# Two-layer convolution and attention kernel: row stores in five pieces, row loads in parts by ScalarE, last stores over three queues

## The chip, the cores and the metric

The kernel runs on one core of one Trainium2 chip. The metric is the device time in microseconds (us) of one execution. All data are float32. The engines are named as in the profile: PE (TensorE, matrix multiplications), DVE (VectorE), ACT (ScalarE), POOL (GpSimd) and SP (SyncE). DMAs are issued by SP, ACT and POOL, each in the order of its own instruction queue.

## The reference

The input x is 2 images of 256 channels and 64 x 64 pixels. Two layers follow each other.

```python
# layer 0: full attention over 4096 pixels, 8 heads of 32 channels, and a masked blend
q, k, v = proj(Wq, bq) / sqrt(32), proj(Wk, bk), proj(Wv, bv)
attn = softmax(einsum('bnd,bmd->bnm', q, k)); fuse = einsum('bnm,bmd->bnd', attn, v)
hybrid = conv1x1(concatenate([x, fuse]), Wf, bf)
x = hybrid * m + x * (1 - m)                      # m: the mask, resized to 64 x 64
# layer 1: a channel gate, attention in 8 x 8 windows, then two grouped convolutions
x = x * sigmoid(relu(x^T ca_w1 + ca_b1) ca_w2 + ca_b2)
x = x + window_attention(x)                       # 4 heads of 64 channels
x = channel_shuffle(x, 4)
y = relu(bn1(conv7x7(x, sa_w1, groups=64)))       # 256 -> 64 channels
y = bn2(conv7x7(y, sa_w2, groups=64))             # 64 -> 256 channels
return x * sigmoid(y)
```

## The kernel before

**Preparation** (some 177 us): projections q, k and v of both images go to DRAM; batch norm is folded into the convolutions' weights, and for each of the 16 *units* (4 of the 64 groups each) a banded weight matrix of 896 KB is built in DRAM (`w_s`).

**Attention** (up to 2674 us): an image is cut into 8 chunks of 512 pixels. For every chunk, two head groups and 32 key blocks give 1024 slots in all. A slot is scores on PE (L666), the exponential on ACT (L679), the product with v on PE (L718), and sums on DVE (L724). When a chunk is through, `stage` runs the rest of layer 0 and the window attention for it, in pieces between later slots. Its last piece adds the result up in `xo` (L1005) and stores its rows to `x_s` in DRAM (L1022). `x_s` holds the rows as the convolutions want them: 3 overlapping blocks of 32 rows per image (`BLOCKS`), 64 groups, 70 columns with the padding.

**Convolutions** (`convolve`): both 7 x 7 convolutions are matrix products with the banded weights. The work list is `items`: 26 pairs of a unit and the images that it takes. Items 0 to 9 are units 0 to 8 and 15 of image 0, which need nothing of the last chunk; they run between the pieces of the last chunk's `stage`. Items 10 to 16 are units 2 to 8 of image 1, items 17 to 22 are units 9 to 14 of both images (the *two-image units*), and items 23 to 25 are units 15, 1 and 0 of image 1.

One step k of the loop at the end of `convolve` is: `conv1(k + 1)`, `conv2(k)`, `gate(k)`, the loads of rows for a later item (`load_rows`), `store(k)`, and sometimes a load of weights (`load_w`). The order on each engine is that of the code.
- `conv1` of a one-image item: 56 matmuls (L1162), then a relu on ACT (L1170).
- `conv1_pairs` of a two-image item: 88 matmuls (L1125) that use sums of neighbouring weights (`both`) and differences of neighbouring columns (`dx`). The first matmuls have `both` as weights. ACT copies the middle sum out (L1136), DVE makes the two results (L1137, L1138), ACT does the relu (L1140).
- `differences(k + 1)` comes at the end of every `conv1(k)`: if the next item takes two images, DVE computes its `dx` from its rows (L1097) and its `both` from its weights (L1102).
- `conv2`: 112 matmuls (L1193) into two PSUM pairs of three, a tanh (L1204) and a scaling copy (L1212) on ACT for each image into a buffer z (four buffers).
- `gate`: z times x on DVE (L1224).
- `store`: 12 DMAs an image from z to the output (L1253; 24 KB or 16 KB each), dealt over queues by the list `engines`. Those for ACT are put in `held` and issued behind the next conv2's copies (L1251). Row loads that wait in `queue` go out on SP between the stores (L1249).

Rows of an item are loaded into one of six buffers (`xcs`) for items from 10 on. One-image items take three DMAs of 140 KB, two-image items two of 420 KB, all issued by SP. Step 12 asks for item 17's rows, step 13 for item 18's, and so on up to step 16 for item 21's; item 22's are asked for by step 17, itself a two-image step, and go out on SP at once (L1075).

For the last chunk the row stores are dealt over POOL and SP and cut into three ranges of groups: 8 to 20 (units 2 to 4), 20 to 64, 0 to 8. After the first range, `last_rows` loads the rows of items 10 to 12.

## Time and profile before

| | |
|---|---|
| median of 3 runs | 2883.06 us (2881.55 to 2884.48) |
| the profiled execution's own time | 2883.86 us |
| its span, from the first to the last instruction | 2882.0 us, mean granted TensorE clock 0.998 |
| busy: PE | 2852.5 us, 99% |
| busy: DVE, ACT, POOL | 2484.3 (86%), 2392.5 (83%), 576.9 (20%) |
| DMA | 305.65 MB, mean 106 GB/s |
| last matmul of attention, of the kernel | about 2674.3, 2868.7 |

Times in the text are us from the span's start. The page gives the busy time of each engine; a stretch of the span can be asked for by itself, and the timeline gives the instructions in order with the idle time before each and what ended it. SPq and ACTq stand for the sequencers of SP and ACT: there the DMA issues are shown, which do not count as busy. When a DMA has landed is told by the semaphore that it raises.

### The profile page before, as it was taken

To read this page: it belongs to the slowest core of one execution; us is meant where nothing else is said; L and a number is where in the kernel's file an instruction comes from. 1 tells how busy PE (TensorE), PEld (TensorE's weight loads), DVE (VectorE), ACT (ScalarE), POOL (GpSimd) and SP (SyncE) were. 2 spreads that over 40 slices of the span, in tenths; PEclk is the share of its full clock that TensorE was granted. 3 is DMA by queue.
4 is the path that set the end of the run, shared out by engine and by line. 5 is a ranking of instruction groups with operands and counts; after the bars stand their busy time and mean duration, and the time that the engine had idled before them with its cause. 6 is when DMAs were issued, how large, how long until landed. Compare 5 with 4: busy or idle time off the path is not lost.

```text
span 2882.0 us, 85464 instructions
## 1 busy us (share of the span) xinstructions
PE 2852.5 (99%) x37198; PEld 831.5 (29%) x37198; DVE 2484.3 (86%) x1374; ACT 2392.5 (83%) x3643; POOL 576.9 (20%) x948
## 2 busy tenths in 40 slices
PE   9999999999999999999999999999999999999998
PEld 4541122222222222222222222222222222222686
DVE  2349999899999999998999999999989899999423
ACT  5569979898888888898989888888989898888434
POOL 7111111111111212121121011111211110000376
PEclk9999999999999999999999999999999999999999
DMA  8555533333343434353333334333434432231675
GB/s 260 202 184 176 154 79 82 94 81 89 74 97 76 109 77 96 87 94 89 85 91 76 88 72 99 76 87 88 101 83 91 93 86 82 64 117 44 188 194 140
DMA packets 245906, 305.65 MB, mean 106 GB/s; under 512 B 121348, under 2 KB 137934, under 8 KB 245266
## 3 DMA queue, kind: packets, MB, share of 16 engines
q1 hardware_dynamic: 200058, 231.43, 28.1%
q0 software_dynamic: 40784, 65.90, 11.9%
q8 instruction: 294, 4.82, 0.7%
q10 hardware_dynamic: 4680, 2.76, 0.4%
q14 instruction: 90, 0.74, 0.1%
HBM read 221.88 MB, written 66.39 MB: 100 GB/s over the span
## 4 chain that ended last, share of the span: by engine, by line
PE 93%; DVE 3%; issue 2%; DMA 1%; POOL 1%; ACT 1%; SPq 0%; ACTq 0%; DVEq 0%; POOLq 0%
PE sa L666 36%; PE ava L718 34%; PE qka L552 4%; PE hya L552 4%; PE v L489 2%; PE c2a L1193 2%; PE vwa L552 2%; PE opa L552 2%; DVE suma L724 2%; PE k L450 2%; PE q L450 1%; PE c1a L1162 1%; PE sca L912 1%; PE oa L974 1%; POOL out_dram L1253 1%
## 5 line engine op out<-in xcount | busy, mean ns | idle before, releaser
L679 ACT ACTIVATE ea<-sa 128x512 f32<-128x512 f32 (+1 forms) x3072 | 2036.4, 747 | 46.3 <-PE sa L666 18.0
L666 PE MATMUL sa<-qa,ka 32*64 32x512 f32 x16384 | 1141.7, 613 | 2.1 <-DVE vst L501 1.7
L724 DVE TENSOR_TENSOR suma<-suma,ea 128x2048 f32<-128x2048 f32 x480 | 1096.4, 2284 | 5.2
L718 PE MATMUL ava<-ea,va 128*32 128x512 f32 x8192 | 1091.0, 605 | 0.3
L724 DVE TENSOR_TENSOR odda<-odda,ea 128x2048 f32<-128x2048 f32 x420 | 959.8, 2285 | 33.1 <-ACT ea L679 33.1
L666 PEld LDWEIGHTS sa<-qa,ka 32*64 32x64 f32 x16384 | 238.8, 129 | 796.6 <-ACT ea L679 728.8
L696 POOL DMA_DIRECT2D folda<-suma x336 | 235.6, 925 | 935.9 <-DVE suma L726 861.3
L718 PEld LDWEIGHTS ava<-ea,va 128*32 128x32 f32 x8192 | 161.4, 108 | 833.3 <-issue 804.3
L1022 POOL DMA_DIRECT2D xs<-xo x98 | 69.5, 718 | 925.3 <-DVE xo L1005 924.2
L1253 POOL DMA_DIRECT2D out_dram<-za x217 | 122.4, 572 | 51.4 <-DVE za L1224 24.5
L552 PE MATMUL qka<-ua,qkv_w 128*32 128x512 f32 x1024 | 115.7, 592 | 0.0
L887 ACT ACTIVATE qka<-qka,qkv_b 128x512 f32<-128x512 f32 x64 | 40.5, 683 | 75.4 <-PE qka L552 75.4
L469 DVE TENSOR_REDUCE top<-sq 128x128 f32<-128x2048 f32 x16 | 36.6, 2286 | 76.0 <-ACT sq L463 76.0
L808 ACT ACTIVATE ta<-hya,bf 128x512 f32<-128x512 f32 x32 | 20.3, 684 | 98.5 <-PE hya L552 98.5
L1193 PE MATMUL c2a<-yca,wa 32*64 32x192 f32 (+1 forms) x2912 | 84.8, 368 | 2.1 <-issue 1.7
L764 POOL DMA_DIRECT2D invs<-inva x62 | 34.8, 570 | 236.2 <-DVE inva L779 234.8
L724 DVE TENSOR_TENSOR suma<-ea,ea 128x2048 f32<-128x2048 f32 x32 | 73.1, 2285 | 7.6 <-ACT ea L679 7.6
L1204 ACT ACTIVATE za<-c2a 128x384 f32<-128x384 f32 x64 | 27.8, 487 | 61.2 <-PE c2a L1193 34.9
L1193 PEld LDWEIGHTS c2a<-yca,wa 32*64 32x64 f32 x2912 | 67.7, 191 | 18.0 <-issue 10.0
L726 DVE TENSOR_TENSOR suma<-suma,odda 128x2048 f32<-128x2048 f32 x30 | 68.8, 2292 | 1.0
L724 DVE TENSOR_TENSOR odda<-ea,ea 128x2048 f32<-128x2048 f32 x30 | 68.5, 2284 | 1.2 <-ACT ea L679 1.2
L552 PE MATMUL hya<-fa,WfT 128*32 128x512 f32 x512 | 59.6, 607 | 2.2 <-DVE fa L785 2.2
(167 smaller groups left out, 1581.1 us busy)
## 6 DMA issues: line engine op xcount, KB each, us to landing
ka<-ks SPq DMA_DIRECT2D x256, 256.0 KB
va<-vs SPq DMA_DIRECT2D x256, 256.0 KB
wa<-ws SPq DMA_DIRECT2D x17, 896.0 KB
ws<-zeros SPq DMA_DIRECT2D x16, 896.0 KB
folda<-suma POOLq DMA_DIRECT2D x224, 64.0 KB, 3.2
folda<-suma POOLq DMA_DIRECT2D x112, 128.0 KB, 4.4
xs<-xo POOLq DMA_DIRECT2D x76, 140.0 KB, 7.1
qs<-qst SPq DMA_DIRECT2D x16, 512.0 KB
```

The costliest lines, as they stand in the source:

```text
L450: nc.tensor.matmul(s[:, g, :], w[:, kc, g * P : (g + 1) * P], rhs, start=(kc == 0), stop=(kc == KC - 1),)
L489: nc.tensor.matmul(sv[:, m, :], xs0[i][:, kc, m * P : (m + 1) * P], wv[:, kc, :], start=(kc == 0), stop=(kc == KC - 1),)
L552: nc.tensor.matmul(out[o : o + 32], weights[:, o : o + 32], x, start=start, stop=stop)
L666: nc.tensor.matmul(heads[j][o], k[r, cols][:, o], q[r, g, :], start=True, stop=not shifted)
L679: nc.scalar.activation(e[:, h, :], tile, AF.Exp, scale=SCALE0)
L696: nc.gpsimd.dma_start(dst[p : p + rows], total[rows * k : rows * k + rows, h, :], accum_op=ALU.add if k else ALU.bypass,)
L718: nc.tensor.matmul(av[r, :], v[:, m % PB, r], e[:, j, :], start=start, stop=stop)
L724: nc.vector.tensor_add(total, first.pop(m % chains, total), e)
L726: nc.vector.tensor_add(acc[1], acc[1], acc[2])
L1022: eng.dma_start(x_s[b, n, p + r0 : p + r1, g0:g1].rearrange("r g w -> g r w"), xo[64 * h + g0 : 64 * h + g1, oc, r0 - WS * c : r1 - WS * c ...
L1193: nc.tensor.matmul(tiles[j // 2][o, j % 2, 0 : n * W], w[r, d, o], y[r, 0:n, d : d + W], start=(d == 0), stop=(d == KS - 1),)
L1253: eng.dma_start(*args)
```

## The change

It has three parts.
1. **Row stores of the last chunk.** The ranges of groups are now 8 to 20, 20 to 36, 36 to 48, 48 to 64 and 0 to 8. The first two are stored at once, with `last_rows` between them as before. The other three wait in `rows_later`, and one is stored behind each of the next three `store` calls (steps 6, 7 and 8 by the timeline of before).
2. **Rows of two-image items.** Where `load_x` put two DMAs into `queue`, it now puts six parts, one per image and block, into `fetch`. `fetch_rows(2)` lets ACT issue two of them at the end of `conv1`, of `conv1_pairs` and of `conv2`; `differences(k)` first has ACT issue what is left of item k.
3. **Last stores.** For the last four items the list of queues is written out letter by letter (g POOL, s SP, a ACT).

```diff
-            parts = [(UG * 2, UG * 5), (UG * 5, NG), (0, UG * 2)] if last else [(0, NG)]
-            for g0, g1 in parts:
+            def store_rows(g0, g1):
                 for oc in range(KC):
...
-                if last and g0 == UG * 2:
-                    staged[0](FIRST + 2)
+            if not last:
+                return store_rows(0, NG)
+            store_rows(UG * 2, UG * 5)
+            staged[0](FIRST + 2)
+            store_rows(UG * 5, UG * 9)
+            for part in ((UG * 9, UG * 12), (UG * 12, NG), (0, UG * 2)):
+                rows_later.append(part)
+            staged.append(store_rows)
...
                     elif len(images) == 2:
-                        queue.append((to, src))
+                        fetch.extend((k, to[:, n], src[:, n]) for n in range(nb))
...
+            def fetch_rows(n, k=-1):
+                while fetch and (n > 0 or fetch[0][0] <= k):
+                    nc.scalar.dma_start(*fetch.popleft()[1:])
+                    n -= 1
...
             def differences(k):
...
+                fetch_rows(0, k)
                 n = B * nb * UG * WP
...
+                fetch_rows(2)                  # conv1_pairs and conv1, ahead of:
                 differences(k + 1)
...
                 while held:
                     held.popleft()()
+                fetch_rows(2)                  # conv2
                 return zs
...
-                engines = (nc.gpsimd, nc.gpsimd, nc.sync)
-                if k == len(items) - 1:
-                    engines = (nc.scalar, nc.sync)
-                elif k == len(items) - 2:
-                    engines = (nc.sync, nc.scalar, nc.sync, nc.gpsimd)
-                elif k >= len(items) - 4 or len(images) == 2:
-                    engines = (nc.gpsimd, nc.sync)
+                last = k - len(items)
+                plan = {-1: "sasasasasass", -2: "sgsasgsasgsa", -3: "gsagsgasgasg", -4: "gsgsagsgsgsa"}
+                plan = plan.get(last, "gs" if len(images) == 2 else "ggs")
+                engines = [{"g": nc.gpsimd, "s": nc.sync, "a": nc.scalar}[i] for i in plan]
...
                 store(k, z, queue)
+                if rows_later:
+                    staged[1](*rows_later.popleft())
```

More of the change, by code (lines that the diff above doesn't have):

```diff
@@ L1033, in pipeline @@
         FIRST = EARLY + 1
-        staged, held = [], deque()
+        staged, held, rows_later, fetch = [], deque(), deque(), deque()
         def convolve():
@@ L1215, in conv2 @@
                     held.popleft()()
+                fetch_rows(2)
                 return zs
```

## The prediction

> **What bounds the kernel now.** I read the page's engine shares first (PE 99% busy), then busy times by stretch of the last 137 us, where all that the diff touches runs, then the timeline there, the waits and the chain. Columns: stretch, us, then busy us (and instructions) of PE, PEld, DVE, ACT, POOL, granted clock, DMA share, GB/s.

> ```profile
> 2745.00:2757.00 12.00, 10.78 (x368) 9.33 (x353) 2.06 (x3) 4.29 (x8) 9.24 (x16) 1.00 0.75 179
> 2757.00:2803.00 46.00, 44.39 (x1391) 38.19 (x1376) 12.99 (x14) 17.66 (x33) 39.52 (x70) 1.00 0.72 201
> 2803.00:2848.00 45.00, 45.00 (x1015) 34.57 (x1003) 20.71 (x27) 19.31 (x37) 28.71 (x51) 1.00 0.70 208
> 2848.00:2869.00 21.00, 20.46 (x624) 16.92 (x616) 5.91 (x8) 11.77 (x25) 19.90 (x36) 1.00 0.37 74
> 2869.00:2882.00 13.00, 0.00 (x0) 0.00 (x0) 1.10 (x3) 1.45 (x5) 1.39 (x3) 0.60 0.26 52
> ```

> TensorE is the bound up to its last matmul at 2868.7. It idles 1.2 us in the first row, 1.6 in the second and 0.5 in the fourth, most of it put down to "issue". In the third row, the two-image items, it never stops: whatever comes late there moves the end by as much. The last 13 us are stores and the exit. So there is little to win: 3.3 us of gaps and a part of the tail.

> The timeline about item 20, a two-image item, shows how short its preparation is:

> ```profile
> 2816.49 5.73 SPq L1253 DMA_DIRECT2D out_dram<-za  x10
> 2816.52 4.87 PE L1193 MATMUL c2a<-yca,wa 32*64 32x384 f32 x112
> 2817.29 1.90 DVE L1097 TENSOR_TENSOR dxa<-xea 128x1679 f32<-128x1679 f32 x1
> 2817.41 0.62 ACT L1140 ACTIVATE yca<-yta,cbias 128x384 f32<-128x384 f32 x1 [1.36 <-DVE yta L1138]
> 2819.11 0.58 DVE L1102 TENSOR_TENSOR botha<-wa 128x384 f32<-128x384 f32 x1
> 2821.32 0.99 PE L1125 MATMUL c1a<-xea,botha 128*32 128x192 f32 x16
> ```

> VectorE makes dx and both for item 20 from its rows (2817.29 to 2819.69, 2.40 in all). TensorE uses both as the very first weights of that item's first convolution, at 2821.32. The slack is 1.6 us. For item 19 it is 2.0 (both ends at 2810.34, PE starts at 2812.34). Now the rows are there many us earlier.

> **Rows by ScalarE.** For items 17 to 21, six parts of 140 KB each replace two SP loads of 420 KB. They enter `fetch` at steps 12 to 16, and two leave behind each conv1 and each conv2, four a step, from step 13. By the end of step 16, 16 of 30 have left: items 17 and 18 and four parts of 19. So:
> - the last two of 19 leave behind the relu of 18 (step 17), just ahead of differences(19);
> - of 20, two leave after conv2(17), two behind the relu of 19, and the last two are forced there by differences(20);
> - of 21 likewise behind the relu of 20.

> VectorE's subtraction needs all six parts. Those of 17 and 18 are out a whole conv half earlier or more; I cost them at nothing.

> When does the last part land? ScalarE's sequencer runs ahead: its event waits for the next instruction begin at 2817.42, as the relu starts. SP issues of such a part last 0.34 to 0.42; with 0.05 between, the fourth starts 1.3 after the relu, the second 0.45. Semaphore updates in the trace give the landing of SP's 140 KB loads: 2.15 at least (2730.89 to 2733.04), 2.2 to 2.75 with little beside, 3.5 to 4.1 beside stores and other loads, 5.6 to 7.1 behind an 896 KB weight load. The chain has one:

> ```profile
> 2702.90 3.27 DMA xea<-xs
> ```

> Counting from the end of the previous item's first convolution, TensorE wants the next after 4.73 us (2816.59 to 2821.32).
> - Item 19: relu +0.46 (2807.61 to 2808.07), second part +0.45, landing 4.3 (between 2.15 and 6.4, since SP has just sent 896 KB of weights and 840 KB of rows, on another queue), dx and both +2.40: 7.6, a stall of 2.9.
> - Item 20: +0.82, +1.3, landing 2.6 (only 24 KB stores beside it), +2.40: 7.1, a stall of 2.4.
> - Item 21: the same with landing 3.0 (the tail of item 23's load beside it): 7.5, a stall of 2.8.

> Sum +8.1. With 2.15 for every landing it is 0.7 + 2.0 + 2.0 = 4.7; with 6.4 for item 19 and 4.1 for the others 5.0 + 3.9 + 3.9 = 12.8. Behind VectorE's wait stand the gates of 17 to 19: gate(18) would start at 2823.7 instead of 2823.23, and only stores wait for it.

> [...]

> The issues themselves: 30 x 0.42 = 12.6 us of ScalarE's sequencer. Two behind a pair's last copy run under that copy (0.85). Up to four behind a relu (1.7) fall into the 3.4 to 3.8 us in which ScalarE waits for conv2. Cost 0; without this cover up to 12.6. SP loses ten issues (some 6 us in 2777 to 2801), where it had idle time: 0.

> **A wait that may come with them.** SP and ACT share eight landing semaphores in the trace, and an issue waits until the one eight before it has landed. At the start of the kernel this holds ScalarE up:

> ```profile
> 25.62 0.34 ACTq L477 DMA_DIRECT2D out_b<-in_out_b_dram  x1
> 28.80 1.26 ACT L460 ACTIVATE qst<-q,bq 128x512 f32<-128x512 f32 x2 [5.37 <-DMA out_b<-in_out_b_dram]
> ```

> By the times of before SP has issued five of its twelve stores at 2817.41, and the eighth before is a load that landed by 2816.3: no wait, 0. If all twelve count ahead of the fetch, its fourth part waits for the ninth store, landed at 2822.45: +3.8 for item 20 and again for 21.

> **Rows of the last chunk.** 12 DMAs become 20: POOL and SP get four more each. POOL: 4 x 0.65 (rows 0.57 to 0.73) = 2.6 us, spread over steps 6 to 8. POOL is busy 39.5 of 46 us there; behind it stand the output stores, and z has four buffers, so one is wanted again some 20 us later. SP: 4 x 0.3 to 1.2, with idle time behind. Item 13's rows are still stored at once, those of 17 on by step 8. Cost 0 to +1. The other way: PE's 1.22 us "issue" gap at 2754.4 lies beside the landing of the old burst (SP's row stores took 5.1 to 6.5); it may shrink. The three 420 KB loads beside it stay, so I take half: -0.6 (-1.2 to +1).

> **Last stores.** For the last four items SP has 30 stores now and 27 after, POOL 21 and 18, ACT 9 and 15.

> ```profile
> 2859.82 16.07 SPq L1253 DMA_DIRECT2D out_dram<-za  x28
> 2871.01 6.01 ACTq L1251 DMA_DIRECT2D out_dram<-za  x8
> ```

> SP runs without a break until 2875.9, and its own exit (2.7 to its first wait, 1.7 idle between two waits) sets the end; ScalarE's exit is done 1.4 earlier. SP's 3 issues less at 0.48 are -1.4. But SP and ACT together issue one per 0.38 here, each waiting for a landing eight back, and together they have three more: +1.1. ScalarE's four issues behind the eviction of 23 take 1.7 us from 2861.5; the relu of 25 started at 2863.1 and is wanted, 0.4 long, at 2865.6. I take -0.5 (-1.4 to +1.5). [...]

> **Sum.** +8.1 - 0.6 - 0.5 = +7.0. The profiled execution took 2883.86 (span 2882.0 and 1.9 around it), 0.8 above the median of 2883.06; on the median the forecast is 2890.1.

> **Rivals.**
> - *Not slower: the parts are early enough.* If the last parts of each item land before the slack is used up, no stall is left, and tail and gap give -1.1 to -2.6: about 2881. The point of decision: item 20's last part landed by 2818.9 (2821.3 less 2.40), 0.2 after its fourth issue. The fastest row is 2.15, so it needs half a step more of lead than I count. 5%, of which 2 reach the bound for faster.
> - *Short stalls.* Landings near 2.15 and the full gains: 4.7 - 2.6 to 4.7 + 1.0, 2885 to 2888.8. For it: ScalarE's queue is otherwise empty, so no weight load is ahead of the parts. Against: DMA share 0.70. 25%.
> - *The shared landings bind.* 8.1 + 7.6 - 1.1 = +14.6: 2897.7. For it: the start of the kernel. Against: the count of five stores. 18%.
> - My forecast, stalls of 7 to 11 us: 2888.9 to 2894, 52%.

> The measurement can tell about 0.2% (5.8 us) from no change. Faster by more would need 2877.3, almost all that gaps and tail hold, with no stall: 2%. Within 0.2%: 28%. Slower: 70%. The range 2885 to 2898 leaves out the first rival and more than a full lane wait.

> **What would show it.** Right: in the two-image stretch TensorE has three gaps of 2 to 3 us ahead of L1125 of items 19, 20, 21, released by VectorE's both, and VectorE's dx (L1097) waits on the DMA of the rows; none ahead of 17, 18 and 22. ScalarE issues thirty row parts, with no idle of its own behind them. Wrong: stretch still full of PE, or gaps elsewhere; ScalarE's evictions (L1204) waiting on row DMAs (third rival); a tail from the last matmul to the end that is not 12.3 to 14.8 us (13.3 now).

## The result and the profile after

The changed kernel took a median of 2899.68 us (2896.44 to 2903.76, six runs), the kernel before beside it 2883.02 (2881.55 to 2886.55, six runs): a ratio of 1.0053, 95% interval 1.0043 to 1.0063. That is slower by 16.7 us. The forecast was slower by 7.0 us, 2890.1, with a range up to 2898.0; the measured median lies above it.

The profiled execution took 2897.57 us, its span is 2895.8. The busy times by stretch, in the columns used above (last four: granted clock, DMA share, GB/s after the engines):

```profile
2745.00:2757.00 12.00, 10.26 (x336) 9.11 (x336) 1.52 (x3) 4.29 (x8) 9.98 (x18) 1.00 0.71 173
2757.00:2803.00 46.00, 43.82 (x1390) 38.74 (x1386) 13.80 (x15) 17.68 (x33) 39.77 (x71) 1.00 0.68 182
2803.00:2848.00 45.00, 33.48 (x645) 24.27 (x644) 15.20 (x20) 13.10 (x25) 21.89 (x40) 0.85 0.62 183
2848.00:2869.00 21.00, 21.00 (x488) 15.28 (x476) 6.78 (x9) 8.68 (x17) 13.01 (x24) 1.00 0.45 115
```

Most of the loss is in the third row, the two-image items. PE was busy 45.0 of 45.0 us there and is now busy 33.5, with 645 matmul records in place of 1015. The 11.5 us of idle time are not the whole: the granted clock has fallen from 1.00 to 0.85, so the remaining matmuls are longer too.

The timeline of PE gives the gaps, each ahead of the first convolution of a two-image item. The bracket holds the idle time before the instruction and what ended it; only the first matmuls of each item are shown:

```profile
2800.40 1.36 PE L1137 MATMUL c1a<-xla,botha 128*32 128x192 f32 x24 [1.29 <-ACT za L1218]
2815.05 2.16 PE L1137 MATMUL c1a<-xla,botha 128*32 128x192 f32 x24 [5.64 <-DVE botha L1114]
2828.98 2.17 PE L1137 MATMUL c1a<-xea,botha 128*32 128x192 f32 x24 [3.33 <-DVE botha L1114]
2841.98 1.76 PE L1137 MATMUL c1a<-xea,botha 128*32 128x192 f32 x24 [2.55 <-ACT za L1218]
2852.43 1.35 PE L1137 MATMUL c1a<-xla,botha 128*32 128x192 f32 x24
```

These are items 18 to 22, with gaps of 1.29, 5.64, 3.33, 2.55 and none: 12.8 us. Three of them were forecast, at 2.9, 2.4 and 2.8; the one ahead of item 18 was not. The first and fourth line name ACT as releaser, but VectorE's `both` ended within 0.1 us of PE's start there as well (item 18: 2799.74 and 0.56 long, PE at 2800.40). The first 24 matmuls take 1.35 us for item 22 and 2.16 for item 19 with the same shapes: that is the clock.

Where item 19's `both` was late, the timeline of all engines shows (the first line is the issue of item 20's first two parts):

```profile
2811.99 0.81 ACTq L1096 DMA_DIRECT2D xea<-xs  x2
2812.57 1.91 DVE L1109 TENSOR_TENSOR dxa<-xla 128x1679 f32<-128x1679 f32 x1 [7.56 <-DMA xla<-xs]
2814.40 0.55 DVE L1114 TENSOR_TENSOR botha<-wa 128x384 f32<-128x384 f32 x1
```

VectorE is idle for 7.56 us ahead of `dx`, which waits for rows, then makes `dx` and `both`, and PE starts at once. The chain of waits goes through the same DMA:

```profile
2800.40 3.13 PE c1a L1137 x62
2805.43 7.12 DMA xla<-xs
2812.57 0.07 DVE dxa L1109
```

The row part that ScalarE issued at 2805.43 landed 7.12 us later. The landing of the last part of each item, from the semaphore updates in the trace, with its issue: item 18 2791.99 and 5.90, item 19 2805.43 and 7.12, item 20 2822.65 and 3.72, item 21 2836.45 and 2.86.

The granted clock, asked for stretch by stretch, falls to one half at three of the gaps. The first three rows below are such stretches, the fourth lies between two of them:

```profile
2811.94:2818.76 6.82, 3.71 (x48) 2.62 (x52) 4.12 (x4) 0.86 (x2) 2.65 (x5) 0.50 0.26 66
2829.00:2832.42 3.42, 3.42 (x44) 2.45 (x48) 1.61 (x2) 0.07 (x1) 2.38 (x5) 0.50 0.94 317
2842.66:2846.07 3.41, 3.41 (x51) 2.87 (x47) 1.04 (x2) 0.20 (x1) 3.03 (x6) 0.50 0.64 193
2818.76:2829.00 10.24, 6.91 (x164) 4.75 (x156) 3.22 (x5) 4.19 (x8) 4.10 (x8) 1.00 0.59 164
```

The first convolutions of items 19, 20 and 21 take 5.79, 5.65 and 5.71 us for it, where item 22's takes 4.20 and those of the kernel before 4.25: 1.5 + 1.4 + 1.5 = 4.4 us.

At the end, the last conv2 waits for the relu of item 25, and that stands behind ScalarE's four stores of item 22:

```profile
2875.11 4.56 ACTq L1263 DMA_DIRECT2D out_dram<-za  x4
2879.72 0.42 ACT L1183 ACTIVATE yca<-c1a,cbias 128x192 f32<-128x192 f32 x1 [4.22 <-DMA out_dram<-za]
2880.19 2.98 PE L1207 MATMUL c2a<-yca,wa 32*64 32x192 f32 x112 [1.41 <-ACT yca L1183]
```

Four issues that should take 1.7 us last 4.56. The third and fourth start at 2878.16 and 2879.36, each within 0.08 us of the last update of the semaphore that it uses: they waited for the landing of an earlier store, 2.0 us in all. The second is 1.30 long, which no semaphore explains. PE waits 1.41 where it waited 0.28. The stores of SP:

```profile
2855.31 33.04 SPq L1265 DMA_DIRECT2D out_dram<-za  x51
```

SP runs without a break until 2888.35. From the last matmul's end (2883.17) to the end it is 12.6 us, 13.3 before.

**The account.** From the last attention matmul to the last matmul it was 194.4 us, and is 210.9: +16.5. Of that the gaps ahead of items 18 to 21 are 12.8, the half clock behind them 4.4, the wait of the last conv2 1.1, together 18.3; the remaining -1.8 are smaller gaps elsewhere, of which I can put none to an edit. With the tail at -0.65 it makes +15.9 behind attention, against 16.7 on the medians (interval 12.4 to 18.2). The two profiled spans differ by 13.8 only, since attention, which the change doesn't touch, ended 2.1 us earlier in the second.

### The profile page after: what moved, and what is told of

It reads as the page before. It is cut to its first block, busy times and chain, and to the rows that moved or that the text cites. A ratio compares the mean times of both kernels' runs of the same rounds, so it can differ in the third digit from the quotient of the medians.

```text
span 2895.8 us, 85471 instructions
## 1 busy us (share of the span) xinstructions
PE 2854.9 (99%) x37198; PEld 833.6 (29%) x37198; DVE 2484.6 (86%) x1374; ACT 2392.6 (83%) x3643; POOL 577.1 (20%) x949
## 4 chain that ended last, share of the span: by engine, by line
PE 92%; DVE 3%; issue 2%; DMA 2%; POOL 1%; ACT 1%; SPq 0%; DVEq 0%; ACTq 0%; POOLq 0%
PE sa L666 35%; PE ava L718 34%; PE qka L552 4%; PE hya L552 4%; PE v L489 2%; PE vwa L552 2%; PE opa L552 2%; DVE suma L724 2%; PE c2a L1207 2%; PE k L450 2%; PE q L450 1%; PE c1a L1175 1%; PE sca L912 1%; POOL out_dram L1265 1%; PE oa L974 1%
```

## The experiments

The first four kernels ran on one chip (kernel before there: 2885.82 median, 25 runs), the second four on another (2886.94, 15 runs). So the ratios are compared, not the times. The theory: ScalarE's parts leave too late, VectorE's `dx` waits, PE idles, and the idling halves the clock. The rivals: another of the three parts costs the time; the lead is enough and something else is late; the clock has no part in it.

### Each part alone

Row stores only: the other two parts as before.

```diff
-                        fetch.extend((k, to[:, n], src[:, n]) for n in range(nb))
+                        queue.append((to, src))
...
-                plan = {-1: "sasasasasass", -2: "sgsasgsasgsa", -3: "gsagsgasgasg", -4: "gsgsagsgsgsa"}
+                plan = {-1: "as", -2: "sasg", -3: "gs", -4: "gs"}
```

> The kernel before with only the row stores of the last chunk in five pieces. Theory A (the last parts of items 18 to 21 come late, and that is nearly the whole loss): 2883, within 2 us of the kernel before, no gap ahead of L1137 of items 18 to 21. Theory B (the pieces themselves or their queues cost several us): 2887 or more.

Measured: 2883.86, ratio 0.9994 (0.9985 to 1.0004). There is no gap ahead of items 18 to 21. From attention to the last matmul 196.0 us, tail (from there to the end) 13.9.

Row fetch by ScalarE only: three ranges of row stores and the old list of queues.

```diff
-            store_rows(UG * 5, UG * 9)
-            for part in ((UG * 9, UG * 12), (UG * 12, NG), (0, UG * 2)):
-                rows_later.append(part)
-            staged.append(store_rows)
+            store_rows(UG * 5, NG)
+            store_rows(0, UG * 2)
...
-                plan = {-1: "sasasasasass", -2: "sgsasgsasgsa", -3: "gsagsgasgasg", -4: "gsgsagsgsgsa"}
+                plan = {-1: "as", -2: "sasg", -3: "gs", -4: "gs"}
```

> The kernel before with only the two-image rows in parts by ScalarE. Theory A: +14 to +17 us over the kernel before, from gaps of 1.3, 5.6, 3.3 and 2.6 us ahead of items 18 to 21 (12.8 in all) and half a clock behind three of them (4.4). Theory B: less than +8, the rest being in the row stores and the last stores.

Measured: 2900.11, ratio 1.0051 (1.0034 to 1.0068), that of the whole change. The timeline of PE in this kernel has the same four gaps (line numbers are two lower):

```profile
2804.74 1.36 PE L1135 MATMUL c1a<-xla,botha 128*32 128x192 f32 x24 [1.58 <-ACT za L1224]
2818.75 2.17 PE L1135 MATMUL c1a<-xla,botha 128*32 128x192 f32 x24 [5.00 <-DVE botha L1112]
2833.38 1.34 PE L1135 MATMUL c1a<-xea,botha 128*32 128x192 f32 x24 [3.18 <-DVE botha L1112]
2846.30 1.34 PE L1135 MATMUL c1a<-xea,botha 128*32 128x192 f32 x24 [2.41 <-DVE botha L1112]
```

Together 12.2 us. The granted clock is 0.5 for 6.8 us about item 19 and for 3.4 us in item 20, and stays full behind the gap of 2.41.

Last stores only:

```diff
-            store_rows(UG * 5, UG * 9)
-            for part in ((UG * 9, UG * 12), (UG * 12, NG), (0, UG * 2)):
-                rows_later.append(part)
-            staged.append(store_rows)
+            store_rows(UG * 5, NG)
+            store_rows(0, UG * 2)
...
-                        fetch.extend((k, to[:, n], src[:, n]) for n in range(nb))
+                        queue.append((to, src))
```

> The kernel before with only the new deal of the last stores. Theory A: the relu of the last item is held up by ScalarE's four held stores of item 22 and TensorE waits some 1.4 us for it, the tail gives back 0.6: +0 to +1.5 us. Theory B (the deal over three queues is what costs): +5 or more. The mechanism hoped for (SP ends earlier): -1.4.

Measured: 2885.40, ratio 0.9997 (0.9988 to 1.0007). PE waits 0.79 us for the last relu (0.28 before) and the tail is 11.1 us (13.3 before): the one loses and the other gains on this profile, and the sum can't be told from nothing.

So parts 1 and 3 are each within 0.15% of no change, and part 2 alone gives the whole loss.

### Twice the lead

The parts leave four at a time, so that all are out well before they are wanted.

```diff
-                fetch_rows(2)
+                fetch_rows(4)
...
-                fetch_rows(2)
+                fetch_rows(4)
...
-                fetch_rows(2)
+                fetch_rows(4)
```

> The changed kernel, but ScalarE issues four parts behind each convolution in place of two, so that each two-image item's rows are out a whole item earlier; the same 30 parts, bytes and queues. Theory A (lateness): the four gaps and the clock loss go, 2881 to 2886, some 15 us below the changed kernel. Theory B (ScalarE's issues or their shared landing semaphores are what costs): still 2892 or more.

Measured: 2884.43, ratio 0.9994 (0.9984 to 1.0003). The two-image stretch of this kernel is nearly full of PE, at full clock (columns as above):

```profile
2797.00:2843.00 46.00, 44.51 (x1012) 34.90 (x1016) 23.43 (x31) 19.51 (x37) 30.67 (x55) 1.00 0.73 220
```

No gap over 0.2 us is left ahead of items 18 to 21, with the same thirty issues on ScalarE and the same bytes. Landings of 6.5 to 7.3 us occur here too (three parts issued at 2807.25 to 2808.09); they cost nothing. So it is the lead, not the number of DMAs and not ScalarE's issue time. The end got worse: the relu of item 25 stands behind the held stores for longer.

```profile
2864.70 3.20 ACTq L1263 DMA_DIRECT2D out_dram<-za  x4
2867.95 0.42 ACT L1183 ACTIVATE yca<-c1a,cbias 128x192 f32<-128x192 f32 x1 [6.41 <-DMA out_dram<-za]
2868.43 5.17 PE L1207 MATMUL c2a<-yca,wa 32*64 32x192 f32 x112 [3.59 <-ACT yca L1183]
```

A wait of 3.59 us, and the clock is 0.5 behind it: the last conv2 takes 5.17 us, 2.98 in the kernel with the change.

### PE kept busy through the gaps

Six matmuls on constants, into a buffer that the convolution then overwrites, ahead of the first convolution of items 19 to 21. They leave twelve records: every matmul of the convolutions leaves two as well (44 of a two-image item's first convolution leave 88).

```diff
                 last = avp.tile([P, CH], F32, tag="av", name=f"c1o{arm}{k}")
+                for _ in range(6 if k in (19, 20, 21) else 0):
+                    nc.tensor.matmul(
+                        last[:, 0:256], ones, keysum.rearrange("p g i h -> p (g i h)"),
+                        start=True, stop=True,
+                    )
```

> The changed kernel with six matmuls of 128x256 on constants, into a PSUM tile that is overwritten afterwards, ahead of the first convolution of items 19, 20 and 21: they run in the gaps, nothing else changes. Clock theory (the granted clock of 0.5 behind a gap makes these convolutions 5.7 us long in place of 4.25): at least items 20 and 21 are back at 4.3 and the kernel is 2.5 to 4.4 us faster than the changed one. Rival (they are long because their operands come from SBUF beside the landing rows): still 5.7, no faster.

Measured: 2897.24, ratio 1.0039 (1.0024 to 1.0054). Item 19 in this kernel's timeline of PE:

```profile
2813.23 2.86 PE L1127 MATMUL c1oa<-keysum,ones 128*128 128x256 f32 x12
2817.49 1.46 PE L1142 MATMUL c1a<-xla,botha 128*32 128x192 f32 x24 [1.40 <-ACT za L1231]
```

The row of busy times from the added matmuls into item 19's first convolution, in the same kernel, gives the clock of 1.00:

```profile
2813.20:2820.40 7.20, 5.80 (x84) 5.14 (x80) 4.12 (x4) 3.32 (x6) 1.85 (x4) 1.00 0.23 59
```

The rows arrive no earlier: 2.86 us of added work and 1.40, 0.88 and 1.31 us of idle time fill the places of the gaps (12.2 us in all), but the first matmuls take 1.46 and 1.36 for items 19 and 20, and no half clock follows in items 19 to 21 (the same row for 20 and 21 has 1.00 too). It follows once, behind a gap of 1.80 ahead of item 18, which had no added matmuls. That the clock's fall comes from PE's idling is shown by the profile. The time went the same way, but the intervals of this kernel and the change overlap.

### The next rows after the stores

At step 17 SP sends item 22's rows (840 KB) just ahead of item 19's last parts. Here it sends them behind the stores of that step.

```diff
-                if xcs:
+                if xcs and k != EARLY + 8:
...
                 store(k, z, queue)
+                if k == EARLY + 8:
+                    load_rows(k + 5)
```

> The changed kernel with item 22's two row loads of 420 KB by SP issued behind the stores of step 17 in place of ahead of them, so that only the 896 KB of weights stand beside the last two parts of item 19. Theory (bytes beside them made these parts land 7.1 us after their issue): 3.5 to 5, the gap ahead of item 19 falls from 5.6 to 2.5 to 4, the kernel gets 2 to 4 us faster. Rival (ScalarE's queue is slow by itself): gap still over 5.

Measured: 2899.48, ratio 1.0045 (1.0030 to 1.0061). PE's timeline, items 18 to 21:

```profile
2805.60 2.16 PE L1137 MATMUL c1a<-xla,botha 128*32 128x192 f32 x24 [1.98 <-ACT za L1226]
2818.34 1.36 PE L1137 MATMUL c1a<-xla,botha 128*32 128x192 f32 x24 [1.18 <-ACT za L1218]
2831.24 1.66 PE L1137 MATMUL c1a<-xea,botha 128*32 128x192 f32 x24 [3.89 <-DVE botha L1114]
2844.91 1.70 PE L1137 MATMUL c1a<-xea,botha 128*32 128x192 f32 x24 [3.14 <-DVE botha L1114]
```

Item 19's last parts now land in 2.4 and 2.7 us (6.7 and 7.1 with the change), and its gap falls from 5.64 to 1.18. So ScalarE's queue is not slow by itself: what SP had sent held the parts up. How much of it the 840 KB did is not separated, since item 18 ran at half clock here and SP's 896 KB of weights went out 4.2 us ahead of these parts (1.0 with the change) and landed 0.7 us after the first one's issue. Two other readings say that both count. In the kernel with added matmuls, with the weights 3.6 us ahead and the 840 KB 2.7 and 1.9 us ahead, the same parts took 5.6 and 5.7 us. And item 18's last parts, which no row load of SP's stands beside, took 6.3 and 6.8 us in this kernel, 1.6 and 1.9 us behind the issue of a weight load.

The gaps of items 20 and 21 are greater by 0.6 each, that of item 18 by 0.7; I can put none of the three to the moved load. It was issued at 2828.43, as the last part of item 20 landed (2828.54), and had landed by 2833.5, ahead of the issue of item 21's last four parts; item 18's gap ended at 2805.60, ahead of all this. Gaps 10.2 us and half clock 5.5 us make 15.7, with the change 17.2. A gain is there in the place, and in the time none that can be told from the change's.

### No held stores for item 22

```diff
-                plan = {-1: "sasasasasass", -2: "sgsasgsasgsa", -3: "gsagsgasgasg", -4: "gsgsagsgsgsa"}
+                plan = {-1: "sasasasasass", -2: "sgsasgsasgsa", -3: "gsagsgasgasg", -4: "gs"}
```

> The changed kernel with item 22's stores dealt over GpSimd and SP alone, as before, so that ScalarE has no stores between the evictions of item 23 and the relu of item 25. Theory (the held stores wait for landings of SP's stores and hold that relu up): the 1.4 us wait ahead of the last conv2 falls to 0.3, and the kernel is 1 us faster, or 0 to 1 if SP's longer list gives it back in the tail. Rival: the wait stays.

Measured: 2897.99, ratio 1.0042 (1.0026 to 1.0057). The last conv2 in this kernel:

```profile
2881.51 2.58 PE L1207 MATMUL c2a<-yca,wa 32*64 32x192 f32 x104 [0.29 <-ACT za L1218]
```

The wait is 0.29, as before the change. The wait of 1.41 is therefore item 22's held stores. The gaps at items 19 to 21 are 4.92, 3.45 and 2.55, and none at item 18; that one comes and goes without an edit.

### Both: twice the lead, no held stores

The two edits shown above together: `fetch_rows(4)`, and the list for the fourth last item as before. This was to be the version that beats both kernels.

> Four parts behind each convolution, and item 22's stores over GpSimd and SP alone. In the profile of the run with four parts alone TensorE waited 3.6 us for the last relu and ran at half clock behind it. If the held stores are the cause, both go: 2878 to 2881, 3 to 5 us below the kernel before. If they are not: 2884.

Measured: 2885.19, ratio 0.9994 (0.9985 to 1.0003). The last conv2 waits 0.29, but the tail is 13.4 us, 10.1 in the kernel with twice the lead alone. That the stores take at the end what PE no longer waits for is not shown: in the kernel without held stores and with the old lead the tail is 10.9 us, shorter than with the change (12.6). The expectation was missed, and why stays open: without the stalls the change is worth -0.06%, which can't be told from nothing.

## Why the prediction was wrong in its size and right in its kind

**Right.** The mechanism, the places and the sign. The gaps stand ahead of items 19, 20 and 21, `dx` waits for the DMA of the rows and PE for `both`; the kernel with the fetch alone reproduces the loss, and twice the lead removes it. Item 21's gap was 2.55 for 2.8, its landing 2.86 for 3.0; the issues and the 2.40 of VectorE were as counted, and the relu of items 19 and 20 came 0.36 us sooner than counted (0.46 behind the convolution, not 0.82). That rows and last stores move little was right (-0.6 and -0.5 forecast; alone, neither can be told from nothing), as was the issue time of the row parts at no cost. The tail shrank by 0.65, forecast -0.5, but that agreement is luck: over the profiles tails are 12.3 to 13.9 us with the old list of queues and 10.1 to 13.0 with the new one.

**Wrong.** By the steps of the sum:
- *The landing of item 19's last part*, 4.3 forecast (2.15 to 6.4), measured 7.12, outside its bounds. The gap was 5.64, forecast 2.9: +2.7. The prediction named the 896 KB of weights and 840 KB of rows that SP had just sent on another queue, and took the middle of its bounds. With the rows moved and the weights further ahead the landing was 2.7 us: the other queue was no protection. The rows that fitted were the highest, 5.6 to 7.1 behind a weight load. These were misread: in the trace before they are loads of 420 KB, issued from 2794.53 on; the 140 KB loads next behind a weight load, two microseconds or more after its issue (from 2709.44 and from 2737.22 on), took 3.5 to 4.2.
- *Item 20's landing*, 2.6 forecast, measured 3.72: gap 3.33 for 2.4, +0.9. The four that left together landed 2.17, 2.63, 3.63 and 3.72 us after their issues, the four of item 21 in 2.15 to 2.86. The last two of item 20 lie beside output stores, as the prediction knew; 2.6 was too near the lower end of its rows.
- *Item 18 at nothing*, "out a whole conv half earlier or more". Its last parts left at 2791.62 and 2791.99, a whole half earlier as stated, but landed 4.9 and 5.9 us later beside weight load and stores; `both` ended at 2800.3. +1.3 in this profile, 0 to 2.0 in the other kernels with this lead: the last part landed after 5.0 us in the one without that gap (no held stores), after 6.4 to 6.8 in the three with it.
- *The clock behind the gaps* was not in the sum. In the trace before, the two-image stretch has no idle time and a clock of 1.00, so that stretch gave no price; but a bound on both sides for idling, as for the waits, was due. It is +4.4. The matmuls added in the gaps removed it.
- *The relu of item 25*: costed at nothing with 1.7 us for ScalarE's four stores ahead of it. They took 4.56, 2.0 of it in waits of two issues for landings; +1.1. This is the third rival's mechanism, shared landings. It was looked for in the fetch, where it didn't occur (of the last parts of items 19 to 21 the longest issue is 0.99, the others 0.33 to 0.46), and came at the end.

The errors of these five, 2.7 + 0.9 + 1.3 + 4.4 + 1.1 = 10.4, less 0.25 for item 21, are 10.2. With 1.2 more gained in the small gaps than forecast, and 0.15 in the tail, that is 8.8 on the profiles; on the medians 9.7 were missed. The upper bounds of the terms, 12.8 for all landings late, held the gaps by luck: item 19's excess was offset by items 20 and 21, which stayed below theirs.

The price of idling did stand in the trace before, in another place: from 376.42 on PE is idle for 2.18 us, and from 379.92 on the granted clock is 0.5 for 3.41 us (columns as above):

```profile
376.51:379.92 3.41, 1.32 (x13) 0.42 (x17) 3.41 (x3) 0.00 (x0) 0.00 (x0) 1.00 0.00 0
379.92:383.33 3.41, 3.41 (x22) 0.85 (x16) 3.03 (x2) 0.00 (x0) 0.00 (x0) 0.50 0.00 0
```

The half clock comes in stretches of 3.41, 3.42 and 6.82 us with the change, and in every profile here their starts lie a whole number of 3.413 us apart (2811.94, 2829.00 and 2842.66 above: five and four of them; in the trace before, 379.92 and the fall behind PE's last matmul at 2871.65: 730). The length of a gap alone doesn't tell what follows it: behind one of 2.55 us the clock fell, and in the kernel with added matmuls behind one of 1.80; behind one of 2.55 in the kernel without held stores it did not.

Where the gap falls tells more: cut each span into windows of 3.41 us by these starts, and add up PE's idle time in each. Of the windows that ran at full clock, in all ten profiles, every one with 2.08 us idle or more was followed by the half clock, and of those with 1.75 or less only one (1.60). Of the five between, with 1.77 to 1.87, two were. With the change, the windows that the half clock followed have 2.53, 3.33 and 2.55 us (from 2808.53, 2825.59 and 2839.25 on), and no other full-clock window up to PE's last matmul has over 1.74; before, it followed the one of 2.09 (the first line above: 1.32 busy of 3.41), and the next has 1.77. The gap of 2.55 with the change lies whole in one window; the one without held stores is cut into 0.68 and 1.87 us, and the clock stays full. The windows (of the change, then of the kernel without held stores; busy PE is the first number behind the comma):

```profile
2839.25:2842.66 3.41, 0.86 (x24) 0.71 (x20) 3.17 (x3) 3.13 (x6) 0.00 (x0) 1.00 0.79 262
2843.79:2847.20 3.41, 1.54 (x35) 1.57 (x39) 3.26 (x4) 2.69 (x5) 0.48 (x1) 1.00 0.92 317
```

**Open.** Why the landing of item 18's last part differs between kernels that load alike up to there. How much of item 19's landing was weights and how much rows. And the -1.8 us of small gaps; profiles of kernels that tie in time differ by two to four microseconds from attention's end to the kernel's.

## What to carry to other kernels

A load that is cut up and metered out behind another engine's work must leave one landing under load, and not the median landing, before the step that needs it: here 7.12 us for item 19's last part, where the four of item 21 took 2.15 to 2.86. Look for what the other queues send in those microseconds: with the 840 KB moved on SP and the weights further ahead, item 19's last parts on ScalarE landed in 2.4 and 2.7 us in place of 6.7 and 7.1. Where TensorE has no slack and will idle, price the clock behind the gap too: one gap of 1.80 us already had a half clock behind it here, and with the change the clock cost 4.4 us on 12.8 us of gaps, a third again. Two of ScalarE's four held stores waited 2.0 us for landings, with the last relu behind them; so ask which instruction stands behind DMA issues on a compute engine's queue and when it is wanted.
